# Two more pieces of a weight matrix made by Strassen's products, and the first loads of B^T issued from ScalarE

## The chip, the cores and the metric

The kernel runs on one core of one Trainium2 chip. The metric is the device time of one execution in microseconds. Before the change three runs took 2601.64, 2601.73 and 2603.40 us; the median is 2601.73.

## The reference

Two residual blocks work on x (32 x 128 x 2048, f32). Only the first one's feed-forward layer matters here:

```python
def _L0_ffn_ref(x, W, bias, A, Bf, coeffs, scales):
    out = jnp.einsum('bsd,od->bso', x, W) + bias
    xa = jnp.einsum('bsd,erd->ebsr', x, A)
    w = coeffs * scales
    upd = jnp.einsum('ebsr,eor,e->bso', xa, Bf, w)
    return out + upd
...
x = x + _L0_ffn_ref(_L0_cond_ref(x, ...), W, bias, A, Bf, coeffs, scales)
x = x + _L1_ffn_ref(_L1_cond_ref(x, ...), up, down, perm)
```

W is 2048 x 2048, and the 16 low-rank updates of rank 16 have 256 rows together. They can be folded into the weights: W' = W + B (w A), whose inner size is 256. The rest (a small network that mixes kernels by condition, a grouped convolution, a per-head feed-forward with GELU and a permutation of columns) runs later and isn't touched.

## The kernel before

**W' in pieces.** W' is made once, in 16 pieces of 128 x 2048 elements (1 MB), named by (kh, oh, kc): kh and oh are halves of the input and output dimension, kc one of four groups. A piece is one tile `w_...` with four parts [ki, oi] of 128 x 512. The order is `blocks`: (0,0), (0,1), (1,1), (1,0), each with kc from 0 to 3. For each part, the scaled A (two slabs c of 128 rows) times B^T (the same two slabs) has to be added to W. A and B^T lie in two tiles each, one for each half: `a_sb[h]` and `bf_sb[h]`.

**Two ways to make pieces.** `w_make` makes one piece plainly: four parts, two matmuls of 128 x 512 each (c = 0 and 1) into a PSUM bank, and one VectorE add of the bank to the part (L184), eight matmuls and four adds. `w_make_two` makes two pieces with the same (kh, oh) at once. Seen over c, ki and oi the product is a 2 x 2 by 2 x 2 block product, and it is done with Strassen's seven products (in Winograd's form): seven matmuls for each piece, and after each product an add of the bank to one part (L226), seven for each piece. Three banks for each piece hold running sums, so a later product adds into a bank that VectorE must have read before: P6 adds into the bank that P1 filled. It needs combinations of A (`a_combine`, four subtractions or additions of 128 x 512 on GpSimd, L193 to L196) and of B^T (`b_combine`, four subtractions of 128 x 512 on VectorE, L211, which it hands out one at a time through `part`).

**The order.** The schedule is the program's own order on each engine. It starts with `warm_up` (two matmuls on zeros). SyncE's queue then issues the coefficients (L995), A's first kc (L137, two DMAs), B^T's first quarter in two halves and its second quarter (L149), the rest of A's first half (L137, two DMAs), pieces 0 and 1 of W, the first x tile, pieces 2 and 3, B^T's second half, pieces 4 and 5, A's second half, and so on. VectorE scales A (L145) as it lands. Pieces 0 to 3 are made plainly by `make_first`; while piece 3 is made, `part` puts one of the four combinations of B^T's second half (tb[1]) after each of its adds.

`inner_weights("P1", first, make_first)` drives this. For each kc it calls `make_first(kc)` and then gives GpSimd three subtractions that combine the parts of that piece (L252 to L254). `make_first` also stores the made piece to DRAM from GpSimd's queue (L168), adds one part to a row sum on GpSimd (L1029), and for kc = 2 makes the combinations of the first x tile on GpSimd (L311 to L314). After the loop GpSimd does four more subtractions in place (L256), one for each piece.

**What follows.** `steps` are 7 rounds (P1, P2, P6, P7, P5, P3, P4) of 8 groups of x. In the first round each step makes two more pieces with `w_make_two` (at g = 0 pieces 4 and 5, from tb[1]) and then multiplies one group of x (`multiply`, L349), which reads the four first pieces and GpSimd's combinations of them and of x: its first two products read the pieces as they are, the third and fourth the combinations of L253 and L252, the fifth the result of L256.

All large tiles come from one pool of 24 slots, and PSUM's eight banks from one list, taken from its front and given back at its end.

Of the kernel before, what the change touches and what calls it, by code (L numbers as in the profile page):

```python
# [11 lines left out]
ALU = mybir.AluOpType  # L12
# [7 lines left out]
QW = 512  # L20
# [35 lines left out]
def adaln_ffn_kernel(  # L56
# [16 lines left out]
    nc = tc.nc  # L73
# [8 lines left out]
    def slot(name, shape=(P, L)):  # L82
        return big.tile(list(shape), FP, name=name, tag="s")


    def bank():
        return banks.pop(0)

    def done(*ps):
        banks.extend(ps)  # L90
# [41 lines left out]
    bf_sb = [slot(f"bf_sb{h}", (P, 2, 2, QW)) for h in range(2)]  # L132

    def a_load(h, k0, k1):
        for ki in range(2):
            i0 = (2 * h + ki) * QW
            nc.sync.dma_start(  # L137
                a_sb[h][:, :, ki, k0:k1].rearrange("p c k i -> p c (k i)"),
                A[:, :, i0 + k0 * P : i0 + k1 * P],
            )  # L140

    def a_scale(h, k0, k1):
        for c in range(2):
            cols = a_sb[h][:, c, :, k0:k1]
            nc.vector.tensor_scalar(cols, cols, wsc[:, c : c + 1], None, ALU.mult)  # L145

    def b_load(h, q, o0=0, n=QW):
        i0 = (2 * h + q) * QW + o0
        nc.sync.dma_start(bf_sb[h][:, :, q, o0 : o0 + n], BfT[:, :, i0 : i0 + n])  # L149

    def warm_up():

        t = slot("warm", (P, QW))
        nc.vector.memset(t, 0.0)
        pw = bank()
        for _ in range(2):
            nc.tensor.matmul(pw, lhsT=t[:, 0:P], rhs=t, start=True, stop=True)
        done(pw)

    wsum = slot("wsum", (P, 2, 2, QW))  # L160
# [6 lines left out]
    def w_store(k, t):  # L167
        nc.gpsimd.dma_start(wb_d[k], t.rearrange("p k o c -> p (k o c)"))  # L168

    def w_make(k, t, between=lambda: None):  # L170

        kh, oh, kc = k
        for oi in range(2):
            for ki in range(2):
                pw = bank()

                n = QW // 2 if k == (0, 0, 0) and oi == 0 else QW
                for o0 in range(0, QW, n):
                    for c in range(2):
                        nc.tensor.matmul(  # L180
                            pw[:, o0 : o0 + n], lhsT=a_sb[kh][:, c, ki, kc],
                            rhs=bf_sb[oh][:, c, oi, o0 : o0 + n], start=(c == 0), stop=(c == 1),
                        )
                nc.vector.tensor_tensor(t[:, ki, oi], pw, t[:, ki, oi], ALU.add)  # L184
                done(pw)
                between()
        w_store(k, t)
# [14 lines left out]
    def b_combine(oh, tt):  # L202
        t = slot(f"tb_{oh}", (P, 4, QW))
        b11, b12, b21, b22 = (bf_sb[oh][:, c, oi] for c in range(2) for oi in range(2))
        parts = [
            (t[:, 0], b12, b11), (t[:, 1], b22, t[:, 0]), (t[:, 2], b22, b12), (t[:, 3], b21, t[:, 1])
        ]

        def part():
            if parts:  # L210
                tt(*parts.pop(0), ALU.subtract)  # L211

        return part, {
            "P1": b11, "P2": b21, "P3": b22, "P4": t[:, 3],
            "P5": t[:, 0], "P6": t[:, 1], "P7": t[:, 2],
        }

    def w_make_two(ks, ts, sa, tb):
        pxs, pys, pzs = ([bank() for _ in ks] for _ in range(3))

        def product(n, ps, first, last, ki, oi):
            for (_, _, kc), p, t in zip(ks, ps, ts):
                nc.tensor.matmul(
                    p, lhsT=sa[n][:, kc], rhs=tb[n], start=first, stop=last, skip_group_check=True
                )
                nc.vector.tensor_tensor(t[:, ki, oi], p, t[:, ki, oi], ALU.add)  # L226

        product("P1", pxs, True, False, 0, 0)
        product("P2", pzs, True, True, 0, 0)
        done(*pzs)  # L230
        product("P6", pxs, False, False, 0, 1)
        product("P5", pys, True, False, 1, 1)
        product("P7", pxs, False, False, 1, 1)
        product("P3", pys, False, True, 0, 1)
        done(*pys)
        product("P4", pxs, False, True, 1, 0)
        done(*pxs)
        for k, t in zip(ks, ts):
            w_store(k, t)
# [2 lines left out]
        for ki in range(2):  # L242
            nc.vector.tensor_tensor(wsum[:, oh], wsum[:, oh], t[:, ki], ALU.add)

    def inner_weights(name, ts, between=lambda kc: None):

        t1, t2, t4 = (slot(f"{name}_t{k}", (P, 4, QW)) for k in (1, 2, 4))
        tt = nc.gpsimd.tensor_tensor
        for kc, t in enumerate(ts):
            between(kc)  # L250
            b11, b12, b21, b22 = (t[:, ki, oi] for ki in range(2) for oi in range(2))
            tt(t1[:, kc], b12, b11, ALU.subtract)  # L252
            tt(t2[:, kc], b22, t1[:, kc], ALU.subtract)  # L253
            tt(t4[:, kc], b21, t2[:, kc], ALU.subtract)  # L254
        for t in ts:
            tt(t[:, 0, 1], t[:, 1, 1], t[:, 0, 1], ALU.subtract)  # L256
        return {
            "t4": t4,
            "P1": [t[:, 0, 0] for t in ts], "P2": [t[:, 1, 0] for t in ts],
            "P3": [t[:, 1, 1] for t in ts], "P7": [t[:, 0, 1] for t in ts],  # L260
            "P4": [t4[:, kc] for kc in range(4)], "P5": [t1[:, kc] for kc in range(4)],
            "P6": [t2[:, kc] for kc in range(4)],
        }
# [594 lines left out]
    def small():  # L858
# [131 lines left out]
    blocks = [  # L990
        (kh, oh, kc) for kh, oh in ((0, 0), (0, 1), (1, 1), (1, 0)) for kc in range(4)
    ]
    steps = [(r, g) for r in ROUNDS for g in range(NG)]
    warm_up()
    nc.sync.dma_start(cs, coeffs)  # L995
    nc.vector.tensor_tensor(wsc, cs[:, 0:2], cs[:, 2:4], ALU.mult)
    a_load(0, 0, 1)
    a_scale(0, 0, 1)
    b_load(0, 0, 0, QW // 2)
    b_load(0, 0, QW // 2, QW // 2)  # L1000
    b_load(0, 1)
    a_load(0, 1, 4)
    a_scale(0, 1, 4)
    wt = {k: w_load(*k) for k in blocks[0:2]}
# [8 lines left out]
    lhs, sa, tb = {}, {}, {}  # L1013
    sa[0] = a_combine(0, nc.gpsimd.tensor_tensor)
    first = [wt.pop(k) for k in blocks[0:4]]

    part, tb[1] = b_combine(1, nc.vector.tensor_tensor)

    def make_first(kc):
        t = first[kc]  # L1020

        if kc == 3:
            w_make(blocks[kc], t, part)
        else:
            w_make(blocks[kc], t)
        made.append(blocks[kc])
        if kc == 2:
            lhs[0] = x_combine(*steps[0], xs.pop(0))
        nc.gpsimd.tensor_tensor(wsum[:, 0, 1], wsum[:, 0, 1], t[:, 0, 1], ALU.add)  # L1029

    rhs = inner_weights("P1", first, make_first)
    a_load(1, 0, 4)
    unsummed, unsummed_first = [], list(first)
    olds = {}
    chain = small()
    nxt, waiting, ts = {}, {}, {}
# [6 lines left out]
    for i, (r, g) in enumerate(steps):  # L1043
# [18 lines left out]
        if g == NG - (1 if ri else 2) and ri < len(ROUNDS) - 1:  # L1062
            nxt = inner_weights(ROUNDS[ri + 1], [nxt[kc] for kc in range(4)])
# [35 lines left out]
        def between(j):  # L1099

            b = (ri - 1) * (NG - 2) + g + 1 if ri > 0 else g - (NG - 2)
            if (g in range(1, NG - 1) if ri > 0 else g >= NG - 2) and b < B and j < KEXP // 2:
                mixed_kernel(b, (2 * j, 2 * j + 1))
            if ri == 0 and j == 2:
                for k in blocks[6 + 2 * g : 8 + 2 * g]:
                    wt[k] = w_load(*k)
            if r in THIRD and j < 4 and quarter_ops:
                nc.vector.tensor_tensor(*quarter_ops.pop(0), ALU.subtract)
            if j == 3 and ahead and steps[i + 2][0] == "P6":
                xs[i + 2] = x_loads(*steps[i + 2])  # L1110
            if ri == 0 and j in (1, 3) and unsummed:
                row_sums(*unsummed.pop())
            if ri == 0 and j == 5 and unsummed_first:
                t = unsummed_first.pop(0)
                tt = nc.vector.tensor_tensor
                tt(wsum[:, 0, 0], wsum[:, 0, 0], t[:, 0, 0], ALU.add)
                tt(wsum[:, 0], wsum[:, 0], t[:, 1], ALU.add)
            if last_round:
                if j == 3 and i + 1 < len(steps):
                    lhs[i + 1] = x_combine(*steps[i + 1], xs.pop(i + 1))  # L1120
                    olds_load(i + 1)
                if j in (2, 4):
                    stage(k0 + j // 2, stage_first)
                if j % 2:
                    stage_third(k0 + j // 2)
                else:
                    stage(k0 + j // 2, stage_second)
# [18 lines left out]
        if g == NG - 1 and ri + 1 < len(ROUNDS):  # L1146
            rhs = nxt
# [3 lines left out]
    for k, (g, h) in enumerate(heads):  # L1151
# [5 lines left out]
        t = ts.pop(k)  # L1157
# [75 lines left out]
```

## Time and profile before

| | |
|---|---|
| median of three runs | 2601.73 us |
| the profiled execution | 2603.33 us, its span 2601.6 us |
| TensorE busy | 2582.1 us (99%) |
| VectorE busy | 1476.3 us (57%) |
| GpSimd busy | 1322.5 us (51%) |
| ScalarE busy | 533.6 us (21%) |
| first multiplication starts at | 49.83 us of the span |

The profile is one execution. Times in it count from the span's start. PE is TensorE's matmuls, PEld its weight loads, DVE VectorE, ACT ScalarE, POOL GpSimd and SP SyncE; SPq and POOLq rows are DMA issues on those queues. An f32 matmul leaves two records. L12 is line 12 of the kernel. A timeline row gives start, length, engine, line, operation, what it writes and reads, how often, and in brackets the engine's idle time before it and what ended that. The row of a stretch gives each engine's busy time, then the granted TensorE clock, the busy share of the 16 DMA engines and GB/s.

### The profile page before, as it was taken

The page shows a single profiled execution, that of the slowest core. Times are in us where ns is not written, and L with a number is a line of the kernel's source. Part 1 is how long each engine was busy: PE and PEld are TensorE (multiplying, and loading weights), DVE is VectorE, ACT ScalarE, POOL GpSimd, SP SyncE. Part 2 cuts the span into 40 slices and gives each one's busy share as a digit, 9 for nine tenths or more (in the row PEclk, how much of TensorE's full clock was granted, in tenths as well). Part 3 has the DMA queues.
Part 4 walks back from the last instruction along what each step waited for, and adds up shares of the span by engine and source line. Part 5 has one row for each costly group of instructions (what it writes and reads, how often), then busy time and mean ns, then how long its engine had stood idle before and what let it go on. Part 6 is the DMA issues. An engine that isn't in the chain of part 4 may idle for free. (4 is left out here: it accounts for less than half of the span.)

```text
span 2601.6 us, 21348 instructions
## 1 busy us (share of the span) xinstructions
PE 2582.1 (99%) x6876; PEld 1304.0 (50%) x6876; DVE 1476.3 (57%) x2326; ACT 533.6 (21%) x1099; POOL 1322.5 (51%) x1092
## 2 busy tenths in 40 slices
PE   9999999999999999999999999999999999999998
PEld 4444455455455555555454544555545555455543
DVE  5554465356455676544276666667666666666610
ACT  0000000000000000000011244444444444444432
POOL 7321657888986854967323234343444334434232
PEclk9999999999999999999999999999999999999999
DMA  7542458688557487474767797877777877787532
GB/s 311 221 162 99 188 194 331 262 335 324 209 227 290 185 322 299 194 311 162 249 214 259 227 308 260 254 235 226 226 235 236 257 234 222 224 253 236 166 117 89
DMA packets 188160, 608.28 MB, mean 234 GB/s; under 512 B 17680, under 2 KB 92944, under 8 KB 144016
## 3 DMA queue, kind: packets, MB, share of 16 engines
q1 hardware_dynamic: 149936, 473.74, 51.3%
q0 software_dynamic: 32704, 130.04, 14.9%
q10 hardware_dynamic: 5408, 3.13, 0.4%
q8 instruction: 55, 0.90, 0.1%
q14 instruction: 57, 0.47, 0.1%
HBM read 372.45 MB, written 200.84 MB: 220 GB/s over the span
## 5 line engine op out<-in xcount | busy, mean ns | idle before, releaser
L818 PE MATMUL bank<-t,ws 128*128 128x512 f32 x1024 | 460.4, 592 | 0.0
L829 PE MATMUL bank<-gl,ws 128*128 128x512 f32 x1024 | 460.2, 592 | 0.0
L836 POOL DMA_INDIRECT out<-t,orow x128 | 151.0, 1180 | 543.8 <-DVE t L834 482.2
L821 ACT ACTIVATE gl<-bank 128x512 f32<-128x512 f32 x512 | 306.5, 599 | 445.2 <-PE bank L818 435.4
L829 PEld LDWEIGHTS bank<-gl,ws 128*128 128x128 f32 x1024 | 194.6, 190 | 233.0 <-issue 231.0
L818 PEld LDWEIGHTS bank<-t,ws 128*128 128x128 f32 x1024 | 194.5, 190 | 226.9 <-issue 223.0
L567 POOL TENSOR_TENSOR x<-x,fb 128x512 f32<-128x512 f32 x128 | 176.4, 1407 | 224.8 <-DMA x<-in_x 153.8
L834 DVE TENSOR_TENSOR t<-bank,t 128x512 f32<-128x512 f32 x128 | 88.5, 691 | 320.4 <-PE bank L829 320.4
L573 ACT ACTIVATE bank<-w,aggb 128x512 f32<-128x512 f32 x128 | 81.0, 684 | 872.9 <-DMA w<-w_d 855.6
L439 PE MATMUL bank<-P_t,s_P 128*128 128x512 f32 x544 | 241.8, 592 | 0.0
L435 DVE TENSOR_TENSOR u<-bank,u 128x512 f32<-128x512 f32 x168 | 110.7, 688 | 196.2 <-PE bank L439 178.1
L283 POOL TENSOR_TENSOR xt<-xt,xt 128x512 f32<-128x512 f32 x128 | 161.9, 1297 | 106.1 <-DMA xt<-in_xT 88.2
L311 POOL TENSOR_TENSOR s_P<-xt 128x512 f32<-128x512 f32 x56 | 73.3, 1308 | 254.9 <-DMA xt<-in_xT 185.2
L439 PE MATMUL bank<-wo_P,s_P 128*128 128x512 f32 x448 | 199.1, 592 | 0.0
L546 DVE SCALAR_TENSOR_TENSOR ags<-mix,att_bc,ags 128x128 f32<-128x128 f32 x224 | 184.8, 825 | 4.7
L439 PEld LDWEIGHTS bank<-P_t,s_P 128*128 128x128 f32 x544 | 103.4, 190 | 115.6 <-issue 112.4
L802 POOL DMA_INDIRECT t<-hx_d,row x128 | 131.8, 1030 | 53.1 <-issue 25.1
L349 PE MATMUL bank<-P_t,s_P 128*128 128x512 f32 x352 | 154.7, 592 | 0.0
L439 PEld LDWEIGHTS bank<-wo_P,s_P 128*128 128x128 f32 x448 | 85.1, 190 | 95.2 <-issue 92.6
L674 PE MATMUL bank<-va,tw_l 128*128 128x256 f32 x512 | 122.0, 380 | 1.0 <-DVE va L658 1.0
L342 DVE TENSOR_TENSOR u<-bank,u 128x512 f32<-128x512 f32 x84 | 56.4, 685 | 110.0 <-PE bank L349 108.6
L674 PEld LDWEIGHTS bank<-va,tw_l 128*128 128x128 f32 x512 | 96.8, 190 | 43.1 <-issue 32.4
(188 smaller groups left out, 3591.5 us busy)
## 6 DMA issues: line engine op xcount, KB each, us to landing
xt<-in_xT SPq DMA_DIRECT2D x88, 1024.0 KB
u<-u_d SPq DMA_DIRECT2D x40, 1024.0 KB
wo_P<-wb_d SPq DMA_DIRECT2D x36, 1024.0 KB
u<-c_d SPq DMA_DIRECT2D x64, 512.0 KB
x<-in_x SPq DMA_DIRECT2D x32, 1024.0 KB
xg<-x SPq DMA_DIRECT2D x256, 128.0 KB
hx_d<-x1t SPq DMA_DIRECT2D x32, 1024.0 KB
hx_d<-ht SPq DMA_DIRECT2D x32, 1024.0 KB
```

What stands on the lines that cost most here:

```text
L283: nc.gpsimd.tensor_tensor(out[:, i, j], a[:, i, j], b[:, i, j], op)
L349: nc.tensor.matmul(ps, lhsT=lhs[k][:, bass.ts(kc, P)], rhs=rhs[k][kc], start=first and kc == 0, stop=last and kc == 3, skip_group_check=True,)
L435: nc.vector.tensor_tensor(acc[:, si, oi], ps, acc[:, si, oi], ALU.add)
L439: nc.tensor.matmul(ps, lhsT=lhs[k][:, bass.ts(kc, P)], rhs=rhs[k][kc], start=first and kc == 0, stop=last and kc == 3, skip_group_check=True,)
L546: nc.vector.scalar_tensor_tensor(ag, mix[:, k], att, ag, ALU.mult, ALU.add)
L567: nc.gpsimd.tensor_tensor(xt[:, f], xt[:, f], late["fb"][:, f], ALU.add)
L674: nc.tensor.matmul(out, lhsT=w[:, 2 * i + r], rhs=rhs, start=first and r == 0, stop=last and r == 1, skip_group_check=True,)
L802: nc.gpsimd.indirect_dma_start(out=t.rearrange("p k t -> p (k t)"), out_offset=None, in_=hx_d[g].rearrange("l k t -> l (k t)"), in_offset= ...
L818: nc.tensor.matmul(pu, lhsT=w[:, m * P : (m + 1) * P], rhs=t[:, 0], start=True, stop=True)
L821: nc.scalar.activation(gl[m], pu, AF.Gelu)
L829: nc.tensor.matmul(pd, lhsT=w[:, (MC + m) * P : (MC + m + 1) * P], rhs=gl[m], start=(m == 0), stop=(m == MC - 1),)
L836: nc.gpsimd.indirect_dma_start(out=out, out_offset=bass.IndirectOffsetOnAxis(ap=orow[:, g, h : h + 1], axis=0), in_=t[:, 1], in_offset=None,)
```

## The change

Pieces 2 and 3 are no longer made one after the other with `w_make`, but together with `w_make_two`, from combinations of A's and B^T's first halves (sa[0], which existed, and a new tb[0]). The four combinations of tb[0] are put after the four adds of piece 1; those of tb[1], which stood between the adds of piece 3, now follow the new pair's last add in one block. The pair's two stores and its work on GpSimd move behind the pair's end, and the row sums of pieces 2 and 3 behind all combinations of the four pieces, ahead of the in-place subtractions. The three loads of B^T's first half are issued from ScalarE's queue, at the program's start, instead of SyncE's. tb[0] is still made again in step g = 3, as before.

```diff
--- before.py
+++ after.py
@@ -144,9 +144,9 @@
             cols = a_sb[h][:, c, :, k0:k1]
             nc.vector.tensor_scalar(cols, cols, wsc[:, c : c + 1], None, ALU.mult)
 
-    def b_load(h, q, o0=0, n=QW):
+    def b_load(h, q, o0=0, n=QW, eng=nc.sync):
         i0 = (2 * h + q) * QW + o0
-        nc.sync.dma_start(bf_sb[h][:, :, q, o0 : o0 + n], BfT[:, :, i0 : i0 + n])
+        eng.dma_start(bf_sb[h][:, :, q, o0 : o0 + n], BfT[:, :, i0 : i0 + n])
 
     def warm_up():
 
@@ -242,7 +242,7 @@
         for ki in range(2):
             nc.vector.tensor_tensor(wsum[:, oh], wsum[:, oh], t[:, ki], ALU.add)
 
-    def inner_weights(name, ts, between=lambda kc: None):
+    def inner_weights(name, ts, between=lambda kc: None, after=lambda: None):
 
         t1, t2, t4 = (slot(f"{name}_t{k}", (P, 4, QW)) for k in (1, 2, 4))
         tt = nc.gpsimd.tensor_tensor
@@ -252,6 +252,7 @@
             tt(t1[:, kc], b12, b11, ALU.subtract)
             tt(t2[:, kc], b22, t1[:, kc], ALU.subtract)
             tt(t4[:, kc], b21, t2[:, kc], ALU.subtract)
+        after()
         for t in ts:
             tt(t[:, 0, 1], t[:, 1, 1], t[:, 0, 1], ALU.subtract)
         return {
@@ -992,13 +993,13 @@
     ]
     steps = [(r, g) for r in ROUNDS for g in range(NG)]
     warm_up()
+    b_load(0, 0, 0, QW // 2, nc.scalar)
+    b_load(0, 0, QW // 2, QW // 2, nc.scalar)
     nc.sync.dma_start(cs, coeffs)
     nc.vector.tensor_tensor(wsc, cs[:, 0:2], cs[:, 2:4], ALU.mult)
     a_load(0, 0, 1)
     a_scale(0, 0, 1)
-    b_load(0, 0, 0, QW // 2)
-    b_load(0, 0, QW // 2, QW // 2)
-    b_load(0, 1)
+    b_load(0, 1, eng=nc.scalar)
     a_load(0, 1, 4)
     a_scale(0, 1, 4)
     wt = {k: w_load(*k) for k in blocks[0:2]}
@@ -1014,21 +1015,31 @@
     sa[0] = a_combine(0, nc.gpsimd.tensor_tensor)
     first = [wt.pop(k) for k in blocks[0:4]]
 
-    part, tb[1] = b_combine(1, nc.vector.tensor_tensor)
+    part, tb[0] = b_combine(0, nc.vector.tensor_tensor)
+    part1, tb[1] = b_combine(1, nc.vector.tensor_tensor)
 
     def make_first(kc):
         t = first[kc]
 
-        if kc == 3:
+        if kc == 0:
+            w_make(blocks[kc], t)
+        elif kc == 1:
             w_make(blocks[kc], t, part)
-        else:
-            w_make(blocks[kc], t)
+        elif kc == 2:
+            w_make_two(blocks[2:4], first[2:4], sa[0], tb[0])
+            for _ in range(4):
+                part1()
         made.append(blocks[kc])
         if kc == 2:
             lhs[0] = x_combine(*steps[0], xs.pop(0))
-        nc.gpsimd.tensor_tensor(wsum[:, 0, 1], wsum[:, 0, 1], t[:, 0, 1], ALU.add)
-
-    rhs = inner_weights("P1", first, make_first)
+        if kc < 2:
+            first_sums(kc)
+
+    def first_sums(*kcs):
+        for kc in kcs:
+            nc.gpsimd.tensor_tensor(wsum[:, 0, 1], wsum[:, 0, 1], first[kc][:, 0, 1], ALU.add)
+
+    rhs = inner_weights("P1", first, make_first, lambda: first_sums(2, 3))
     a_load(1, 0, 4)
     unsummed, unsummed_first = [], list(first)
     olds = {}
```

## The prediction

> **What bounds the kernel now.** I read the page's busy table and clock row first.
>
> ```profile
> PE 2582.1 (99%) x6876; PEld 1304.0 (50%) x6876; DVE 1476.3 (57%) x2326; ACT 533.6 (21%) x1099; POOL 1322.5 (51%) x1092
> PEclk9999999999999999999999999999999999999999
> ```
>
> TensorE sets the time: 2582.1 of 2601.6 us, at full granted clock. A change pays only if it takes a matmul away, or shortens a wait of TensorE. Everything it edits runs before the first multiplication, so next come TensorE's waits in the first 60 us and its timeline there.
>
> ```profile
> PE bank L223 <- DVE w L226: 2.5, 1, 2.5
> PE bank L157 <- DVE warm L154: 1.5, 1, 1.5
> PE bank L180 <- DMA bf_sb<-in_BfT: 1.0, 1, 1.0
> PE bank L180 <- DVE a_sb L145: 0.9, 1, 0.9
> ```
> ```profile
> 1.46 3.78 PE L157 MATMUL bank<-warm 128*128 128x512 f32 x4 [1.46 <-DVE warm L154]
> 6.24 7.32 PE L180 MATMUL bank<-bf_sb,a_sb 128*128 128x256 f32 x24 [1.00 <-DMA bf_sb<-in_BfT]
> 14.41 20.87 PE L180 MATMUL bank<-bf_sb,a_sb 128*128 128x512 f32 x48 [0.86 <-DVE a_sb L145]
> 35.12 3.60 PE L223 MATMUL bank<-bf_sb,a_sb 128*128 128x512 f32 x8
> 41.17 5.39 PE L223 MATMUL bank<-tb,sa 128*128 128x512 f32 x12 [2.46 <-DVE w L226]
> 49.83 7.03 PE L349 MATMUL bank<-w,xt 128*128 128x512 f32 x16
> ```
>
> Columns: start, length, engine, line, operation, idle before it and what ended it. Every f32 matmul leaves two records, so the 48 records from 14.41 to 35.12 are 24 matmuls, 0.86 us each. Three gaps lie before the multiplication at 49.83: 1.00, 0.86 and 2.46 us. The last is the existing pair's: its third product adds into a bank whose first product VectorE has not yet added to W, since VectorE is still making B's combinations:
>
> ```profile
> 16.23 4.38 DVE L184 TENSOR_TENSOR w<-bank,w 128x512 f32<-128x512 f32 x7 [1.34 <-DMA w<-in_WT]
> 23.69 0.69 DVE L184 TENSOR_TENSOR w<-bank,w 128x512 f32<-128x512 f32 x1 [1.41 <-DMA w<-in_WT]
> 33.62 1.78 DVE L211 TENSOR_TENSOR tb<-bf_sb 128x512 f32<-128x512 f32 x1 [2.76 <-DMA bf_sb<-in_BfT]
> 35.92 1.15 DVE L211 TENSOR_TENSOR tb<-bf_sb,tb 128x512 f32<-128x512 f32 x1
> 40.35 4.37 DVE L226 TENSOR_TENSOR w<-bank,w 128x512 f32<-128x512 f32 x7
> ```
>
> The landings of W's pieces are the clock of this stretch. VectorE waits for the third at 23.69; SyncE's queue shows the first and the fourth, because each load there waits for an older one's semaphore: the load at 16.15 for the first piece, the one at 28.02 for the fourth.
>
> ```profile
> 5.84 0.60 SPq L164 DMA_DIRECT2D w<-in_WT  x1
> 16.15 0.33 SPq L164 DMA_DIRECT2D w<-in_WT  x1
> 28.02 0.88 SPq L164 DMA_DIRECT2D w<-in_WT  x1
> ```
>
> Today the late fourth piece costs nothing: its first add is due after 31 us. In the changed order it is due at about 25.
>
> **The change, part by part.**
>
> *Matmuls.* Pieces three and four take 7 x 2 = 14 instead of 16: -2 x 0.86 = -1.7 us.
>
> *Earlier loads.* The three B^T issues leave SyncE's queue (L149 took 1.92 us for three), so A's second part goes at 2.57 instead of 4.53 and the first W piece at about 3.9 instead of 5.84; B^T itself starts at 0.74, on a ScalarE that only loads a table then (1.28 us; its next work is at 53). How much earlier does W's stream land? Call it s. Bounds: 0, if the DMA engines are simply full, and 1.96, the shift of the issues. The busy share of the DMA engines by microsecond decides:
>
> ```profile
> 3.00:4.00 1.00, 1.00 (x2) 0.34 (x1) 0.00 (x0) 0.00 (x0) 0.00 (x0) 1.00 0.68 199
> 4.00:5.00 1.00, 1.00 (x2) 0.00 (x0) 0.36 (x2) 0.00 (x0) 0.00 (x0) 1.00 0.82 239
> 7.00:8.00 1.00, 1.00 (x5) 0.68 (x4) 0.00 (x0) 0.00 (x0) 0.00 (x0) 1.00 0.70 183
> 8.00:9.00 1.00, 1.00 (x6) 0.88 (x5) 0.00 (x0) 0.00 (x0) 0.00 (x0) 1.00 0.78 137
> ```
>
> (The last two columns are that share and GB/s.) Free engine time is 0.32 + 0.18 in 3 to 5 us, 0.30 + 0.22 in 7 to 9, about 0.1 in 9 to 10, and some 0.3 of the second microsecond's 0.8: 1.4 us if all is filled, 0.8 if only the ramp is. I take s = 1.1. Then the first piece lands at 15.05, the fourth at 26.9, A's second part at about 12.6.
>
> The Trainium skill (DMA: Bandwidth & Descriptors, section "Issuing engines are not separate DMA queues") says that transfers issued from different engines share the same 16 DMA engines and that a second issuer saves only issue time. This speaks against the edit from 5 us on, where the share is 1.0; if it held from the first microsecond, s would be 0 and the result the third rival's.
>
> *Block one and two.* The first matmul can come when A's first part is scaled (4.64 + 0.35) and the warm-up is over (5.24); sharing the engines with B^T may hold A back, so 5.3 to 6.2 instead of 6.24. The second block needs A's second part scaled: 12.6 + 0.7, so 13.3 instead of 14.41, ending at 20.2. This gain of 1.1 us is only a head start into what follows.
>
> *VectorE in block two and the new pair.* From the first piece's landing: four adds (0.63 apart), then add and combination in turn. In the rows from 33.62 to 40.35 four combinations and three adds took 6.73, so add plus combination is 1.68. The pair's first add comes 2.6 + 4 x 1.68 = 9.3 us after the landing, at 24.4, and a product may follow 0.82 after such an add's start (40.35 to 41.17): 25.2. TensorE has finished the four matmuls of products one and two at 20.2 + 3.4 = 23.6: a new gap of 1.6 us. The next add, for the fourth piece, waits for its landing at 26.9, so the sixth matmul comes at 26.9 + 0.9 = 27.8 instead of 26.1: another 1.7. All VectorE work of the pair stands behind that one add, but adds are 0.63 apart and matmuls 0.86, so it catches up. Nine matmuls (7.7 us) end the pair: landing of the fourth piece + 8.6 = 35.5. Block four ended at 35.12.
>
> *The next pair.* All four combinations of B's second half now follow the new pair's last add. That add starts 0.2 after the pair ends (as 50.03 against 49.83), the first combination 0.6 later, four at 1.1 make 4.4, then the add and 0.82: 6.0 after the pair's end, where it was 41.17 - 35.12 = 6.05. B^T's second half landed at 33.62 and is due at 36.3. So this gap stays: 41.5 instead of 41.17.
>
> *GpSimd.* The pair's two stores now wait for its last add (36.4), and what is queued behind them starts at 37.6 instead of 32.23: four combinations of x (up to 1.72 each), six of the weights (1.35), two sums, four subtractions, ending at 59.6 instead of 54.9. The product that reads the subtractions starts 13.7 after the multiplication's start, at 63.9, so 4 us of cover; without it each microsecond would be paid. GpSimd then waits 22 us for x (until 84.46), where its lateness is gone. The load of the eighth piece now also waits for the first pair's combinations to be read (35.5 instead of 29.84); it is due after 70.
>
> *Sum.* -1.1 (start) - 1.7 (matmuls) + 3.3 (new pair's gaps) - 0.1 (old gap) = +0.4, or by landings: 28.02 - s + 8.6 + 6.0 - 41.17 = 1.45 - s = +0.4 with s = 1.1. The profiled execution took 2603.33 (span 2601.6 and 1.7 around it), so its like would be 2603.7; the median shown is 1.6 lower, and on it I forecast **2602.1 us**.
>
> **The rivals.**
>
> *Faster: VectorE's chain alone binds.* The fourth piece took 4.3 us after the third, the others 2.5, while the first piece's store (issued at 19.99) ran beside it. If that overlap goes, it lands by 25.1 at s = 1.1, the pair ends 1.7 us sooner and the sum is -0.3 - s: -1.4, or **2600.3**; at most -2.3. For it: the loads move and the store's issue depends on GpSimd. Against: the store follows the same stream, since GpSimd's first combinations wait for A's second part.
>
> *Slower: the fourth piece lands late.* Place: the add in front of the sixth matmul of the new pair. Each microsecond later is one paid. It decides from s below 1.45, so a landing after 26.6; with two queues crowding W off until 29.0, s is -1 and the time **2604.2**. To lose over 0.2% (5.2 us) it would have to land after 31.8; the row that lands at 33.62 stands behind 1 MB more, so this is remote.
>
> *The loads do nothing.* s = 0: 1.45 us slower, **2603.2**.
>
> *The clock falls.* The new pair has gaps of 1.6 and 1.7 us with one matmul between. The row against it: the 2.46 us gap before 41.17, with the clock at 1.00 throughout. Price, from the warm-up's four records in 3.78 us where four take 1.72 later: about 2.1 us, so **2604.2** on top of the forecast.
>
> The skill (TensorE: Matmul & The Clock Gate, section "Why this matters for your kernels") warns of idle gaps above about 3 us between matmuls; no single gap here is that long, but the two together are.
>
> **How the numbers follow.** Forecast, 2601.4 to 2602.8: 0.50. Faster rival: 0.22. Loads do nothing: 0.14. Late piece: 0.07. Clock: 0.07. The range 2599.6 to 2604.6 takes in both ends of s, both answers for the fourth piece and the clock's price. A measurement of this kernel tells 0.2%, 5.2 us, from no change. All that could be won is 1.7 us of matmuls and the gaps of 1.00, 0.86 and 2.46 us, with 0.45 us inside the first block (7.32 where 16 half and 8 whole records make 6.87): 6.5 in all, so faster by over 0.2% has 0.04; slower by over 0.2% needs the remote landing, or it with the clock: 0.05. Within: 0.91.
>
> **What would show it.** Right: the wait of L223 for VectorE's adds grows from 2.5 to nearly 6 us in the first 60; the second block starts near 13.3; VectorE waits for a W piece near 26.9 in the middle of the pair; the multiplication starts near 50.2; its later products wait for nothing on GpSimd. Wrong: no wait for the fourth piece (then the faster rival), a second block still at 14.4 (loads do nothing), records of 0.86 pitch after the gaps (clock), or any new wait after 60 us, where the two programs issue the same work in the same order.

## The result, and the profile after

The changed kernel takes 2610.20 us (median of nine runs, 2607.61 to 2611.60) against 2601.73 for the kernel before (nine runs, 2601.56 to 2603.96): the ratio is 1.0029, with a 95% interval of 1.0020 to 1.0037. It is 8.5 us slower, where 0.4 had been forecast. The profiled execution took 2607.61 us, the shortest of the nine; its span is 2605.8.

The page's busy table and clock row, after:

```profile
PE 2582.2 (99%) x6872; PEld 1304.3 (50%) x6872; DVE 1493.3 (57%) x2336; ACT 532.6 (20%) x1099; POOL 1324.5 (51%) x1092
PEclk9999999999999999999999999999999999999999
```

TensorE has four records fewer, the two matmuls saved, and yet the same 2582 us of busy time. So some matmuls have become slower, which the clock row in fortieths of the span is too coarse to show. TensorE's waits in the first 60 us, after:

```profile
PE bank L223 <- DVE w L226: 5.5, 2, 4.0
PE bank L180 <- DVE a_sb L145: 1.6, 1, 1.6
PE bank L157 <- DVE warm L154: 1.5, 1, 1.5
PE bank L180 <- DMA bf_sb<-in_BfT: 0.4, 1, 0.4
```

One wait for VectorE's adds is 4.0 us long. TensorE's timeline after shows where (start, length, idle before and its end, as before):

```profile
6.87 3.72 PE L180 MATMUL bank<-bf_sb,a_sb 128*128 128x256 f32 x16 [1.63 <-DVE a_sb L145]
11.04 10.57 PE L180 MATMUL bank<-bf_sb,a_sb 128*128 128x512 f32 x24 [0.45 <-DMA bf_sb<-in_BfT]
21.44 3.60 PE L223 MATMUL bank<-bf_sb,a_sb 128*128 128x512 f32 x8
26.57 5.41 PE L223 MATMUL bank<-tb,sa 128*128 128x512 f32 x12 [1.54 <-DVE w L226]
35.26 3.60 PE L223 MATMUL bank<-bf_sb,a_sb 128*128 128x512 f32 x8
42.84 7.11 PE L223 MATMUL bank<-tb,sa 128*128 128x512 f32 x12 [3.98 <-DVE w L226]
53.22 7.03 PE L350 MATMUL bank<-w,xt 128*128 128x512 f32 x16
```

Three things are to be seen. The first block of matmuls starts at 6.87, not at 6.24. The new pair (21.44 to 35.26) has the 1.54 us gap of the forecast and ends within 0.15 us of block four before. Then the next pair's third product comes 7.6 us after the pair's start instead of 6.05, behind a gap of 3.98, and the same twelve records that took 5.41 us at 26.57 take 7.11 at 42.84. The multiplication starts 3.39 us later than before: 0.1 us by the pair's end, 1.5 by the longer gap (3.98 against 2.46), 1.7 by the slower records. The other 0.8 us of the 4.2 us between the two spans come after 60 us, where TensorE's waits add up to 5.9 us against 4.9. VectorE in the same stretch, after:

```profile
35.46 0.69 DVE L226 TENSOR_TENSOR w<-bank,w 128x512 f32<-128x512 f32 x1 [0.17 <-PE bank L223]
36.07 0.68 DVE L211 TENSOR_TENSOR tb<-bf_sb 128x512 f32<-128x512 f32 x1
36.78 2.06 DVE L211 TENSOR_TENSOR tb<-bf_sb,tb 128x512 f32<-128x512 f32 x1
38.77 1.74 DVE L211 TENSOR_TENSOR tb<-bf_sb 128x512 f32<-128x512 f32 x1
40.44 1.74 DVE L211 TENSOR_TENSOR tb<-bf_sb,tb 128x512 f32<-128x512 f32 x1
42.10 3.07 DVE L226 TENSOR_TENSOR w<-bank,w 128x512 f32<-128x512 f32 x5
```

The four combinations take 6.0 us, from 36.07 to 42.10. The first takes 0.68, the others 1.74 to 2.06. GpSimd's timeline says what changes between them: up to 37.0 it only issues stores, then it runs the combinations of x, and they are slow too (1.27 us for the first, then 1.6 to 1.7):

```profile
36.45 0.55 POOL L168 DMA_DIRECT2D wb_d<-w  x1 [0.31 <-DVE w L226]
37.01 1.27 POOL L312 TENSOR_TENSOR s_P<-xt 128x512 f32<-128x512 f32 x1
38.37 1.60 POOL L313 TENSOR_TENSOR s_P<-s_P,xt 128x512 f32<-128x512 f32 x1
39.93 1.70 POOL L314 TENSOR_TENSOR s_P<-xt 128x512 f32<-128x512 f32 x1
```

The stretches around the gap, after; the third column from the end is the granted clock:

```profile
40.00:44.00 4.00, 1.16 (x2) 0.58 (x3) 4.00 (x6) 0.00 (x0) 4.00 (x3) 0.92 1.02 432
44.00:48.00 4.00, 4.00 (x7) 1.59 (x6) 2.45 (x4) 0.00 (x0) 3.84 (x4) 0.65 1.01 428
48.00:52.00 4.00, 4.00 (x11) 1.78 (x10) 3.16 (x6) 0.00 (x0) 3.84 (x4) 1.00 0.45 186
```

TensorE is busy all of 44 to 48, but does 7 matmul records there and 11 in the next 4 us. In steps of 0.1 us the clock stands at 0.50 from 43.4 to 46.8.

### The profile page after: what moved, and what is told of

Its sections match the earlier page's. It is cut to its first block, busy times and chain, and to the rows that moved or that the text cites. A ratio compares the mean times of both kernels' runs of the same rounds, so it can differ in the third digit from the quotient of the medians.

```text
span 2605.8 us, 21357 instructions
## 1 busy us (share of the span) xinstructions
PE 2582.2 (99%) x6872; PEld 1304.3 (50%) x6872; DVE 1493.3 (57%) x2336; ACT 532.6 (20%) x1099; POOL 1324.5 (51%) x1092
## 3 DMA queue, kind: packets, MB, share of 16 engines
q10 hardware_dynamic: 6224, 4.18, 0.6%
## 5 line engine op out<-in xcount | busy, mean ns | idle before, releaser
L675 PEld LDWEIGHTS bank<-va,tw_l 128*128 128x128 f32 x512 | 96.9, 190 | 43.4 <-issue 32.2
```

Source lines behind the costliest of these rows:

```text
L675: nc.tensor.matmul(out, lhsT=w[:, 2 * i + r], rhs=rhs, start=first and r == 0, stop=last and r == 1, skip_group_check=True,)
```

## The experiments

All medians are of 10 or 11 runs where nothing else is said, each beside runs of the kernel before on the same chip (medians 2602.0 to 2602.2). Runs of one kernel spread over 2.5 to 6 us, so that differences of about 1 us between two medians are not told from none.

**The pair alone: loads back on SyncE's queue.**

```diff
-    b_load(0, 0, 0, QW // 2, nc.scalar)
-    b_load(0, 0, QW // 2, QW // 2, nc.scalar)
...
-    b_load(0, 1, eng=nc.scalar)
+    b_load(0, 0, 0, QW // 2)
+    b_load(0, 0, QW // 2, QW // 2)
+    b_load(0, 1)
```

> The changed kernel with the three B^T loads back on SyncE's queue: the pair alone. Theory 'block' (the four combinations of tb[1] in one block behind the new pair, slowed by GpSimd's x combinations, hold the next pair's third product some 4 us, and the clock falls after that): nothing of this is undone, and W's fourth piece lands 1.4 us later again (28.02 instead of 26.61), so the next pair's third product comes near 44.2 instead of 42.84 and the time is 1 to 2 us above the changed kernel's 2610, some 2611.5. Rival 'loads' (A's first part landed at 6.46 instead of 4.64 because B^T shares the engines with it, and the late start is what costs): the first block starts at 6.2 again and the time falls to 2602 to 2604.

Measured: 2608.90 us (2606.08 to 2612.03), ratio 1.0027 (1.0018 to 1.0036). The profile has the same gap of 3.99 us, at 44.10. Most of the loss is still there, so "loads" isn't the main cause. But the time isn't 1 to 2 us over the changed kernel's, as the theory "block" has it; it is 1.3 us under, too little to show a price of the loads by itself.

**The loads alone, in the kernel before.** The three B^T loads on ScalarE's queue, pieces three and four made plainly as before.

> The kernel before with only the three B^T loads moved to ScalarE's queue. Theory 'block': the late start (6.9 instead of 6.2) is made good by 14.4 to 14.5, where the second block began before too; B^T's second half lands 1.4 us earlier, so the combinations and with them the pair's third product come earlier, near 39.8 instead of 41.17: 1.0 to 1.4 us faster, 2600.5. Rival 'loads': slower by several us, 2605 to 2609.

Measured: 2604.53 us (2601.04 to 2605.93), ratio 1.0009 (1.0000 to 1.0018), 2.5 us slower, just clear of noise. The theory's 2600.5 missed, and the rival's 2605 to 2609 too. Its profile, of one of the shorter runs (2602.15), shows the pair's third product at 40.49, earlier than the 41.17 before though not at the theory's 39.8, and A's first part landing at 6.33; the longer runs have no profile. The theory "block" alone was too small from here on: moving the loads has a price of its own.

**The block alone, in the kernel before.**

```diff
-            w_make(blocks[kc], t, part)
+            w_make(blocks[kc], t)
+            for _ in range(4):
+                part()
```

> The kernel before with one change: the four combinations of tb[1] stand in one block behind the fourth piece's last add instead of between its adds. No new pair, no moved load. Theory 'block': they start near 35.9 and take 1.1 to 1.75 us each beside GpSimd, so the pair's third product comes at 42 to 43.5 instead of 41.17, a gap of 3.3 to 4.7 us; with the clock falling behind it the time is 2604 to 2609, without a fall 2602.6 to 2604. Rival 'pair' (the new pair's own waits cost): no change, 2601.7 to 2602.5.

Measured: 2605.48 us (2604.17 to 2608.69), ratio 1.0016 (1.0007 to 1.0025). Without any new pair, the place of the four combinations costs 3.4 us. Its TensorE timeline has nearly the same gap and the same slow twelve records as the changed kernel's:

```profile
41.94 7.08 PE L223 MATMUL bank<-tb,sa 128*128 128x512 f32 x12 [3.69 <-DVE w L226]
```

**The block moved to GpSimd, loads as changed.**

```diff
-    part1, tb[1] = b_combine(1, nc.vector.tensor_tensor)
+    part1, tb[1] = b_combine(1, nc.gpsimd.tensor_tensor)
...
-            w_make_two(blocks[2:4], first[2:4], sa[0], tb[0])
             for _ in range(4):
                 part1()
+            w_make_two(blocks[2:4], first[2:4], sa[0], tb[0])
```

> The changed kernel with the four combinations of tb[1] made by GpSimd ahead of the new pair's stores, where it waited 4.55 us for VectorE, instead of by VectorE behind the pair. Theory 'block': the gap of 3.98 us before the next pair's third product is gone, no clock falls there, and the multiplication starts near 47.3 instead of 53.22: 2598 to 2600.5, faster than both kernels. Rival 'loads' or 'pair': the time stays within 2 us of the changed kernel's, 2608 to 2611.

Measured: 2603.75 us (2601.47 to 2605.44), ratio 1.0005 (0.9996 to 1.0014): 6.4 us under the changed kernel, by this edit alone, though short of what was expected. No wait for VectorE's adds is left in its first 60 us. What is left is at the start. VectorE's timeline of this kernel:

```profile
10.62 0.62 DVE L145 TENSOR_SCALAR a_sb<-a_sb,wsc 128x256 f32<-128x256 f32 x2 [8.05 <-DMA a_sb<-in_A]
```

A's first part, which landed at 4.64 before and at 6.46 in the first profile after, lands here at 10.62. TensorE idles 6.1 us there.

**Both undone: the pair with neither the moved loads nor the block.** The last edit together with the first.

> The changed kernel with both remedies: B^T's loads on SyncE's queue, and the combinations of tb[1] on GpSimd ahead of the pair's stores. Theory 'two causes' (the block of combinations costs a gap and a clock fall, and B^T on ScalarE's queue makes A's first part land at 6.3 to 10.6 instead of 4.6): the first block starts at 6.1 in every execution, the new pair ends near 36.5, the next pair runs without a gap and the multiplication starts near 48.5 instead of 49.83: 2600 to 2601.5, under the kernel before. Theory 'block' alone (the loads cost nothing): the same 2603.5 to 2604 as with the loads on ScalarE.

Measured: 2602.58 us (2601.05 to 2604.56), ratio 1.0002 (0.9993 to 1.0011). Putting the loads back gains 1.2 us here, less than expected and within the noise. A's first part lands at 5.51, later than the 4.64 before, with the same order of loads. The multiplication starts at 47.79 and no gap stands before the next pair's third product (TensorE's timeline of this kernel):

```profile
39.21 5.31 PE L223 MATMUL bank<-tb,sa 128*128 128x512 f32 x12
47.79 7.03 PE L350 MATMUL bank<-w,xt 128*128 128x512 f32 x16
```

**A's first part ahead on both queues**, with the combinations on GpSimd.

```diff
-    def a_load(h, k0, k1):
+    def a_load(h, k0, k1, engs=(nc.sync, nc.sync)):
...
-            nc.sync.dma_start(
+            engs[ki].dma_start(
...
-    b_load(0, 0, 0, QW // 2, nc.scalar)
-    b_load(0, 0, QW // 2, QW // 2, nc.scalar)
     nc.sync.dma_start(cs, coeffs)
...
-    a_load(0, 0, 1)
+    a_load(0, 0, 1, (nc.scalar, nc.sync))
     a_scale(0, 0, 1)
+    b_load(0, 0, 0, QW // 2)
+    b_load(0, 0, QW // 2, QW // 2, nc.scalar)
     b_load(0, 1, eng=nc.scalar)
```

> As the changed kernel with the combinations of tb[1] on GpSimd, and with B^T still partly on ScalarE's queue, but A's first part is the first load of both queues (half on each), and B^T's first two halves follow it, one on each queue. If what costs is that B^T's packets stand before A's in the engines, A's first part lands by 4.5 again, the first block starts at 5.3 to 6.2, and W lands a microsecond earlier than with SyncE alone: 2598.5 to 2600.5, the fastest of all. If any load on a second queue costs, 2603 to 2605.

Measured: 2601.19 us (2599.68 to 2603.78), ratio 0.9996 (0.9987 to 1.0005). A's first part lands at 4.18, and the time is 2.6 us under the kernel with B^T first: a second queue doesn't cost by itself, the order does. The edit also puts half of A on each queue; what that alone does wasn't run. The time misses the expected range by 0.7 us, and the first block doesn't start at 5.3 to 6.2, since it now waits for B^T (TensorE's timeline of this kernel):

```profile
7.34 16.92 PE L180 MATMUL bank<-bf_sb,a_sb 128*128 128x256 f32 x40 [2.10 <-DMA bf_sb<-in_BfT]
```

In these profiles what the order takes away is A's late landing (10.15 and 10.62 in two profiles with B^T first), not the wait at the start. The third warm-up matmul's experiment below shows what this wait costs.

**The changed kernel again**, one execution with a profile.

> The changed kernel itself, for a second profile, since nine runs of it spread from 2607.6 to 2611.6 and the profile at hand is of the fastest. Theory 'two causes': what differs between its executions is when A's first part lands (6.46 in the first profile, 10.62 in the kernel with the combinations on GpSimd) and whether the clock falls once or twice before 60 us: a run of 2609 to 2611.6 shows A's first part after 8, or a second stretch of granted clock under 0.9. Theory 'block' alone: the same picture as in the first profile at 2607.6, with only the fall longer.

Measured: 2609.65 us, 2.0 more than the first profiled one. TensorE's timeline and stretches of this execution:

```profile
10.55 16.58 PE L180 MATMUL bank<-bf_sb,a_sb 128*128 128x256 f32 x40 [5.31 <-DVE a_sb L145]
46.68 7.00 PE L223 MATMUL bank<-tb,sa 128*128 128x512 f32 x12 [3.99 <-DVE w L226]
```
```profile
8.00:9.00 1.00, 0.00 (x0) 0.00 (x0) 0.00 (x0) 0.00 (x0) 0.00 (x0) 0.97 1.00 259
9.00:10.00 1.00, 0.00 (x0) 0.00 (x0) 0.00 (x0) 0.00 (x0) 0.00 (x0) 0.50 0.99 374
15.00:16.00 1.00, 1.00 (x4) 0.85 (x3) 0.69 (x1) 0.00 (x0) 0.92 (x2) 0.61 0.96 401
16.00:17.00 1.00, 1.00 (x5) 0.76 (x4) 0.13 (x1) 0.00 (x0) 1.00 (x2) 1.00 1.06 442
```

Here A's first part lands at 10.15, TensorE idles 5.3 us, and the granted clock is 0.50 from 8.9 until 15.8. The gap in front of the next pair is the same 3.99 us, with the same fall behind it. This is the expected picture: what differs between these two executions of the changed kernel is the start; the block costs the same in both.

**GpSimd's tensor work beside the block left out**, loads on SyncE's queue. GpSimd's combinations of the first two x groups, of pieces three and four, their sums and the four subtractions in place are not made; the products of the first round read raw parts of the same size.

```diff
+            if name == "P1" and kc > 1:
+                continue
...
+        if name == "P1":
+            raw = [t[:, 0, 0] for t in ts]
+            return {"t4": t4} | {f"P{n}": raw for n in range(1, 8)}
...
+        if r == "P1" and g < 2:
+            xa[g] = a
+            return {f"P{n}": a[:, 0, 0] for n in range(1, 8)}
```

> The changed kernel with B^T's loads on SyncE's queue, and with GpSimd's tensor work beside the block of combinations left out: the combinations of the first two x groups and of the third and fourth piece, their sums and the four subtractions in place (the products of the first round read raw parts instead, of the same size). If GpSimd's tensor operations are what makes a combination on VectorE take 1.74 instead of 0.68 us, the four take 2.5 to 2.9 us instead of 6.0, the gap before the next pair's third product shrinks from 3.99 to 0.5 to 1.2, the clock stays up, and the multiplication starts near 49.3 instead of 54.5: 2602.5 to 2604.5. If the block's length has another reason, 2607 to 2610 as with GpSimd's work.

Measured: 2603.66 us (2601.21 to 2605.74), 5.2 under the same kernel with GpSimd's work. VectorE and TensorE in its timelines:

```profile
37.46 0.68 DVE L211 TENSOR_TENSOR tb<-bf_sb 128x512 f32<-128x512 f32 x1
38.18 0.69 DVE L211 TENSOR_TENSOR tb<-bf_sb,tb 128x512 f32<-128x512 f32 x1
38.79 0.68 DVE L211 TENSOR_TENSOR tb<-bf_sb 128x512 f32<-128x512 f32 x1
39.39 0.68 DVE L211 TENSOR_TENSOR tb<-bf_sb,tb 128x512 f32<-128x512 f32 x1
```
```profile
40.73 5.42 PE L223 MATMUL bank<-tb,sa 128*128 128x512 f32 x12 [0.48 <-DVE w L226]
```

The block takes 2.5 instead of 6.0 us, the gap is 0.48 instead of 3.99, and the twelve records take 5.42 instead of 7.11: the clock stays up. In the same profile the combinations of tb[0], where GpSimd's work stands as before, still take 1.15 to 2.69 us. The length of the block is GpSimd's doing.

**A third matmul on zeros in the warm-up**, with A first on both queues and the combinations on GpSimd.

```diff
-        for _ in range(2):
+        for _ in range(3):
             nc.tensor.matmul(pw, lhsT=t[:, 0:P], rhs=t, start=True, stop=True)
```

> The kernel with A's first part ahead on both queues and the combinations of tb[1] on GpSimd, and a third matmul on zeros in the warm-up. In the profiles where TensorE idled from 5.24 to 6 or 7, the first block's matmuls then ran at half rate up to 11 us (sixteen matmuls of the first two blocks took 16.8 instead of 13.7 us in the kernel without the third one), although the granted clock's column stays at 1.00. If the idle time behind the warm-up is what leaves the clock low, the third matmul fills it and 1.5 to 3 us go: 2598 to 2600, clearly under both kernels. If the rate is set by something else (the loads, the weights), 2601 to 2603.

Measured: 2599.92 us (2598.51 to 2601.15), ratio 0.9991 (0.9982 to 1.0000): 1.3 us under the same kernel with two, 2.3 us under the kernel before, and the lowest median of all. The groups of the first 50 us by form (busy us and mean ns of one) show the sixteen half-size records of the first block with two warm-up matmuls, and then with three:

```profile
L180 PE MATMUL bank<-bf_sb,a_sb 128*128 128x256 f32 x16 | 6.6, 603 | 2.1 <-DMA bf_sb<-in_BfT 2.1
```
```profile
L180 PE MATMUL bank<-bf_sb,a_sb 128*128 128x256 f32 x16 | 3.7, 384 | 0.4 <-DMA bf_sb<-in_BfT 0.4
```

**The third warm-up matmul alone, in the kernel before.**

> The kernel before with the third warm-up matmul alone. If the low clock at the start is also what spreads the runs before (2600.8 to 2605.2), its slower ones go: 2600.5 to 2601.5. If the start of the kernel before is warm in most runs already, the third matmul delays the first block by up to 0.7 us: 2602 to 2603.

Measured: 2603.24 us (2600.39 to 2604.55), ratio 1.0006 (0.9997 to 1.0015): no gain (1.0 us more, within the noise), and the spread stays. In the kernel before, the start isn't what spreads the runs, or the third matmul gives back what it gains; the runs don't tell which.

**The changed kernel with only the order of the first loads mended.** A first on both queues, the block on VectorE as changed.

> The changed kernel with only the order of the first loads mended: A's first part first on both queues, then B^T. The block of combinations stays on VectorE behind the pair. Theory 'two causes', and each with its own price: the 1.3 to 2.6 us of the loads go and the 6.4 us of the block stay, 2607 to 2608.5, with the gap of 4.0 us before the next pair's third product in the profile. If the two are one cause (a late start pushes the pair against GpSimd's work), the gap shrinks too and the time is under 2605.

Measured: 2607.93 us (2605.28 to 2609.34), ratio 1.0021 (1.0012 to 1.0030), 2.3 us under the changed kernel. A's first part lands at 3.94, and the gap before the next pair is still 3.99 us, with 8.06 us for the twelve records behind it. The two causes are separate, each with its price. Here too TensorE first waits 2.1 us for B^T, until 7.29.

**Both causes in one table**, medians in us, a row for the start and a column for the place of the four combinations, all with the new pair:

| first loads | block on VectorE | on GpSimd | difference |
|---|---|---|---|
| B^T on ScalarE, ahead of A (as changed) | 2610.20 | 2603.75 | 6.4 |
| all on SyncE (as before) | 2608.90 | 2602.58 | 6.3 |
| A first on both queues | 2607.93 | 2601.19 | 6.7 |

The differences along the rows, and between the first and the last row (2.3 and 2.6), are clear of noise; those of 1.0 to 1.4 us between neighbouring rows are not, taken one by one.

## Why the prediction was wrong

*What bounds the kernel, matmuls saved.* Right: TensorE has four records fewer, and no long wait is new after the first multiplication (the longest is 1.5 us, on GpSimd's L395, which was 1.4 before).

*How much earlier W's stream lands.* Right: VectorE's first add of a W piece starts at 14.89, and the load behind the fourth piece is issued at 26.61; 15.05 and 26.9 were forecast. s was 1.3 to 1.4, not 1.1. So the stream did move, and the rival in which the loads do nothing is out.

```profile
14.89 3.17 DVE L184 TENSOR_TENSOR w<-bank,w 128x512 f32<-128x512 f32 x5 [1.33 <-DMA w<-in_WT]
26.61 0.33 SPq L164 DMA_DIRECT2D w<-in_WT  x1
```

*Block one and two.* Wrong in a bound. "5.3 to 6.2 instead of 6.24" had A's first part at worst as late as before. SyncE issues it at 1.19, 0.45 us behind ScalarE's first B^T load, and it landed at 6.46, 10.15 and 10.62 in three profiles with this order, at 6.33 in a fourth, at 4.64 before and at 3.94 to 4.18 with A first on both queues. The price is 2.5 us without the pair and 2.3 to 2.6 against the mended order; the 1.2 to 1.3 against loads on SyncE with the pair are within the noise. The second block didn't start at 13.3 either: it follows the first one at about 14.5, where it began before (14.41), though A's second part is scaled from 12.41 on. That is the sign given for "the loads do nothing", with another cause: the first block began late and waited 0.45 us more for B^T. Holding A back was seen as a possibility and priced at nothing, since the start was taken as "only a head start into what follows", with the fourth piece's landing bounding the stretch. So it is in the first profile (the pair ends at 35.26 all the same), but not where A lands at 10.15 (the pair ends at 39.09).

*The new pair.* The numbers are right in the first profile: a gap of 1.54 us (forecast 1.6), an end at 35.26 (forecast 35.5). The gap is partly luck: TensorE was through with products one and two at 25.0 instead of 23.6, and VectorE's first add of the pair came at 25.75 instead of 24.4, both some 1.4 us late. VectorE was late since its combinations took 1.28, 2.68, 1.15 and 1.15 us here; and the 6.73 us of the forecast's rows hold four combinations but three adds, so that 1.68 for a combination and an add was too little on average even there. The second gap of 1.7 us didn't come, since VectorE was ready for the fourth piece's add only as it landed.

*The next pair.* This is the step that failed: "the first combination 0.6 later, four at 1.1 make 4.4 ... So this gap stays: 41.5". They took 6.0 us and the third product came at 42.84. The 1.1 was read from rows in which every combination alternated with an add from PSUM. In one block against GpSimd's tensor operations they take 1.74 to 2.06 each, and alone 0.68, as the kernel without GpSimd's work shows; the block alone, put into the kernel before, takes 1.64 to 1.75 each after its first. So the row was of the right operation and the wrong neighbours.

*The clock.* The rival was named with a fair price, 2.1 us, but only at the new pair's two short gaps, and with a chance of 0.07. It came behind the next pair's gap, which the step above had made too short: 3.98 us idle, then 1.7 us lost on twelve records (7.11 against 5.41): half of the 3.4 us at a clock of 0.50. The block's price of 6.3 to 6.7 us is these two: 3.99 of gap and 1.6 to 2.7 of slow records (7.00 to 8.06 in four profiles, against 5.3 to 5.4), with up to some 0.6 us that the profiles don't assign.

*GpSimd.* Right: it ends the four subtractions at 58.6 (forecast 59.6), no product waits for them, and it waits 21 us for x afterwards.

*The rivals and the chances.* Within 0.2% had 0.91, on the argument that only 6.5 us could be won and that a loss needed a remote landing. That argument bounded the gain by what exists and the loss by what had been thought of. A gap can also grow, and each of the five gaps of 3.69 to 3.99 us in these profiles brought the clock down with it. Most of the loss came by the place of the four combinations, which no rival named.

*Not settled.* The pair with both faults undone is no faster than the kernel before (2602.58 against 2602.02), though it saves 1.7 us of matmuls and its multiplication starts at 47.79. In that profile the first block's half-size records took 6.1 us, as with the low clock, where the kernel before's took 3.9. This slow first block (5.2 to 6.6 us) is in eight of the thirteen profiles, with every order of the loads, so part of what the rows of the table differ by may be its doing. The third warm-up matmul mends this in the one profile of the best version and does nothing for the median of the kernel before, whose profile had no slow first block; why the start is sometimes slow with the same 5.24 us end of the warm-up wasn't found.

## What to carry to other kernels

Take an operation's duration from a row with the same neighbours on the other engines: here one VectorE subtraction takes 0.68 us alone, mostly 1.15 between adds and 1.74 in a block beside GpSimd (at worst 2.7). Work that a later consumer needs should be spread between the adds, or given to an engine that waits, not put in one block between two chains of dependent matmuls. A small load that everything waits for goes first on every queue; a bigger one ahead of it on another queue (here 1 MB against 0.25) let it land 1.7 to 6 us later.

## What the runs showed of the hardware

A GpSimd tensor operation and a VectorE one on two SBUF operands slow each other: 128 x 512 f32 takes VectorE 0.68 us alone and 1.64 to 2.07 in the block beside GpSimd, and GpSimd 1.27 alone and 1.6 to 1.7 beside this block; adds that read PSUM (0.68) weren't slowed. The Trainium skill (GPSIMD Engine Reference, section "Specifications") says that GpSimd shares its SBUF interfaces with VectorE and that VectorE instructions with two SBUF inputs contend; the runs agree and add the price.

In front of the next pair's third product, gaps of 3.69 to 3.99 us (five profiles) were each followed by a granted clock of 0.50, and gaps of 2.41 and 2.46 us (two profiles) by none. The low clock lasted 3.4 us in four of the five (in the changed kernel 43.4 to 46.8) and 6.8 us in the fifth, A first with the block on VectorE (41.2 to 48.0), whose twelve records took 8.06 us. It lasted 6.8 us too in the two profiles where TensorE idled for 5.3 and 6.1 us at the start. It set in 2.5 to 4.7 us after the last matmul's end, so that idle times of equal length cost different amounts. The skill (TensorE: Matmul & The Clock Gate, section "Why this matters for your kernels") advises no idle gap above about 3 us between matmuls; these runs agree, with no fall at 2.46 and one in every profile from 3.69.

At the very start the profile's clock column doesn't tell the speed: it shows 1.00 where the warm-up's records take 1100 ns instead of 592, and where the first block's half-size ones take 603 instead of 384 (A first on both queues, two warm-up matmuls). Whether it is the clock there, no run shows.
